# The last stage of a graph kernel: who weights the expert outputs, when they are loaded back, and what is prepared before the gathers arrive

## The chip, the core and the metric

The kernel runs on one core of a Trainium2 chip. Its engines work side by side and meet through semaphores: TensorE (PE in the profile; PEld is its weight load), VectorE (DVE), ScalarE (ACT), GpSimd (POOL), and SyncE (SP), which here issues plain DMAs. The metric is the time of the whole launch on the device in microseconds (us), lower being better. Before the change it is 2686.47 us, the median of 3 runs (2683.16 to 2688.34).

## What is computed

The reference is a two-layer graph network with 3125 nodes of 256 values each. Each layer is a graph convolution beside an attention-like mixer, and then a feed-forward part with experts. The change lies in the last part of the second layer, where four experts are weighted by a gate that comes from a second graph attention:

```python
def _L1_ffn_ref(x, W_gat, att_src, att_dst, b_gat, ln_gamma, ln_beta, W1, b1, W2, b2, edge_index):
    ...
        ee = jnp.exp(e - e_max[dst])
        denom = jax.ops.segment_sum(ee, dst, num_segments=M)
        alpha = ee / (denom[dst] + 1e-16)
        msg = h[src] * alpha[:, :, None]
        agg = jax.ops.segment_sum(msg, dst, num_segments=M).reshape(M, HEADS * NUM_EXPERTS) + b_gat
        scores = _layernorm(agg, ln_gamma, ln_beta).reshape(M, HEADS, NUM_EXPERTS).mean(1)
        ...
        topk_s, topk_i = jax.lax.top_k(scores, TOP_K)
        w = jax.nn.softmax(topk_s, axis=-1)
        out = jnp.zeros_like(x)
        for ei in range(NUM_EXPERTS):
            g = jnp.where(topk_i == ei, w, 0.0).sum(-1)
            hh = jax.nn.gelu(x @ W1[ei] + b1[ei], approximate=False)
            out = out + g[..., None] * (hh @ W2[ei] + b2[ei])
        return out
...
    x = x + _L1_ffn_ref(_layernorm(x, axis=-1)[None], ...)[0]
```

So at the end every node has four expert outputs of 256 values, a gate of four numbers (two of them zero), and its old value `x`; the result is `x` plus the gated sum.

## The kernel before

**Tiles.** The 3125 nodes are 25 tiles of 125 rows (`P`, `NT`). The tiles are handled in seven chunks, `CHUNKS`: four of four tiles and three of three. `self.x` holds all of `x` on chip for the whole kernel.

**Ahead of the tail.** `layer1_ffn` computes the four experts one after the other (`expert`, L1704). The outputs of experts 0 and 1 stay on chip (`y[0]`, `y[1]`, the second in the memory of `acc`); those of experts 2 and 3 are stored to `yd` in DRAM. Beside the experts, the segment sums of the graph attention are made by scans over the sorted edges and stored to `sums` in DRAM. After the last expert a short dependent piece (L1819 to L1856) works out what is carried from one partition to the next and leaves it in `taken`.

**The tail, L1859 to L1914,** has these parts:

- Loads (L1864 to L1868): for each of the seven chunks, a tile `yback` gets the outputs of experts 2 and 3 from `yd`. `move` (L63) splits each transfer in two DMAs, of 112 and 13 partitions, so there are 28 DMAs, all on SP's queue, into seven buffers.
- Gathers (L1869): 25 indirect DMAs by GpSimd, one per tile, fetch each node's row of 24 numbers from `sums` into `rs` (called `g_r` in the profile).
- Gates (L1872, and `graph_gates`, L1987): small VectorE operations over all tiles of a group at once, with three trips to ScalarE (exponentials, square root, exponential). There are three groups: chunks 0 and 1 (8 tiles), chunks 2 and 3 (8 tiles), chunks 4 to 6 (9 tiles). Before each group, TensorE fills `more` with the carried parts, one product per tile (L1877). `graph_gates` is a generator and yields at each trip to ScalarE, so that other work can be put there.
- Totals (L1881): `total(k, gate, ta)` adds the gated expert outputs of chunk k to `x`, and stores the chunk. It does so in two ways. Tiles at even places in the chunk are done by VectorE with four operations `x = out * gate + x` (L1889). Tiles at odd places are done by TensorE: an identity product brings `x` into PSUM (L1895), ScalarE makes four diagonal matrices with the gate on the diagonal (L1897), TensorE multiplies each with one expert's output onto the same PSUM tile (L1899), and ScalarE copies the result back to `x` (L1900). With four-tile chunks that is two and two, with three-tile chunks two and one: 14 tiles for VectorE, 11 for TensorE and ScalarE.

**The order.** TensorE, VectorE and ScalarE run in the order in which the Python code issues instructions (`manual_schedule`, L1904); SP and GpSimd are placed by the framework's scheduler. The order on each of these three is thereby fixed. The loop at L1906 issues a group's gates, and at each yield one total of the group before: while group 1's gates wait for ScalarE, chunks 0 and 1 are totalled; during group 2's gates, chunks 2 and 3; chunks 4, 5 and 6 follow at the end. ScalarE's queue is thus, for each round: two exponentials, the diagonals and copies of one chunk, square root (with its table load), the diagonals and copies of the next chunk, exponential (with its table load).

**Buffers.** `yback` has one buffer per chunk, `diag` three, the PSUM tile `fph` three. DMAs of SP use eight semaphores in turn, so that each waits until the one eight before it has landed; the gathers likewise.

Of the kernel before, what the change touches and what calls it, by code (L numbers as in the profile page):

```python
# [8 lines left out]
F32 = mybir.dt.float32  # L9
# [3 lines left out]
OP = mybir.AluOpType  # L13
# [5 lines left out]
D = 256  # L19
P = 125  # L20
NT = 25
CHUNKS = ((0, 4), (4, 4), (8, 4), (12, 4), (16, 3), (19, 3), (22, 3))
# [23 lines left out]
BIG = 1e30  # L46
# [3 lines left out]
def gather(nc, out, table, idx):  # L50
    nc.gpsimd.indirect_dma_start(  # L51
        out=out, out_offset=None, in_=table,
        in_offset=bass.IndirectOffsetOnAxis(ap=idx, axis=0))
# [9 lines left out]
def move(queue, out, in_):  # L63


    for s in (slice(0, 112), slice(112, P)):
        queue.dma_start(out[s], in_[s])
# [7 lines left out]
def rows_of(table):  # L75
    return table.rearrange("(t p) d -> p t d", p=P)
# [12 lines left out]
class Kernel:  # L89
# [1564 lines left out]
    def layer1_ffn(self):  # L1654
        nc, tc, a = self.nc, self.tc, self.a
        NE, FC = 4, 4
        R = 24
        C = 25
        with ExitStack() as c:
            big = c.enter_context(tc.tile_pool(name="f1", bufs=1))  # L1660
            ps_a = c.enter_context(tc.tile_pool(name="f1pa", bufs=2, space=PSUM))
# [5 lines left out]
            vec = {n: self.bcast(big, "L1_ffn_" + n) for n in ("b_gat", "ln_gamma", "ln_beta")}  # L1667
            srow = big.tile([P, NT, 20], F32, name="srow")
            row = big.tile([P, NT, 5], F32, name="row0")
            loop = big.tile([P, NT, 4], F32, name="loop")  # L1670
            tabg = self.dram.tile([N, 20], F32, name="tabg")
            tie = self.ties(big, NE, "s")
# [5 lines left out]
            ends = big.tile([128, N], F32, name="g_ends")  # L1678
# [122 lines left out]
            with tc.manual_schedule(engines={mybir.EngineType.DVE}):  # L1801
                step = -(-EC // (NE * len(CHUNKS)))
                sources(3 * step)
                for ei in range(NE):
                    if ei > 0:
                        w = weights(ei)
                    for t0, n in CHUNKS:
# [3 lines left out]
                        done = ei * len(CHUNKS) + CHUNKS.index((t0, n)) + 1  # L1811
# [41 lines left out]
            taken = big.tile([128, C], F32, name="g_taken")  # L1853
# [7 lines left out]
            ga = c.enter_context(tc.tile_pool(name="f1m", bufs=2))  # L1861
            rs = ga.tile([P, NT, R], F32, name="g_r", bufs=1)
            backs = []
            for t0, n in CHUNKS:  # L1864
                back = ga.tile([P, 2, 4, D], F32, name="yback", bufs=len(CHUNKS))
                for i in range(2):
                    move(nc.sync, back[:, i, :n, :], rows_of(yd[i])[:, t0:t0 + n, :])
                backs.append(back)  # L1868
            for t in range(NT):  # L1869
                gather(nc, rs[:, t, :], sums[:], self.seg_at[:, 1, t:t + 1])  # L1870

            def gates(c0, c1):  # L1872

                ta, tb = CHUNKS[c0][0], CHUNKS[c1 - 1][0] + CHUNKS[c1 - 1][1]
                more = ps_a.tile([P, 16, C], F32, name="ln_pt")
                for t in range(ta, tb):
                    nc.tensor.matmul(more[:, t - ta, :], ends[:, t * P:(t + 1) * P], taken, start=True, stop=True)  # L1877
                for gate in self.graph_gates(ga, ta, tb, rs, more[:, :tb - ta, :], loop, srow, vec, tie):
                    yield gate, ta

            def total(k, gate, ta):  # L1881

                t0, n = CHUNKS[k]
                for t in range(t0, t0 + n):
                    outs = [y[ei][:, t, :] if ei < 2 else backs[k][:, ei - 2, t - t0, :] for ei in range(NE)]
                    xs = self.x[:, t, :]
                    if (t - t0) % 2 == 0:
                        for ei in range(NE):
                            nc.vector.scalar_tensor_tensor(xs, outs[ei], gate[:, t - ta, ei:ei + 1], xs,  # L1889
                                                           op0=OP.mult, op1=OP.add)  # L1890
                        continue

                    diag = ga.tile([P, NE, P], F32, name="diag", bufs=3)
                    pm = ps_h.tile([128, 4 * P], F32, name="fph")[:P, :D]
                    nc.tensor.matmul(pm, self.ident[:P, :P], xs, start=True, stop=False)  # L1895
                    for ei in range(NE):
                        nc.scalar.activation(diag[:, ei, :], self.ident[:P, :P], AF.Copy,  # L1897
                                             scale=gate[:, t - ta, ei:ei + 1])
                        nc.tensor.matmul(pm, diag[:, ei, :], outs[ei], start=False, stop=(ei == NE - 1))  # L1899
                    nc.scalar.copy(xs, pm)  # L1900
                move(nc.sync, rows_of(self.out)[:, t0:t0 + n, :], self.x[:, t0:t0 + n, :])


            with tc.manual_schedule(engines={E_.PE, E_.DVE, E_.Activation}):  # L1904
                ready = []
                for c0, c1 in ((0, 2), (2, 4), (4, 7)):  # L1906
                    for gate in gates(c0, c1):
                        if gate[0] is None and ready:
                            total(*ready.pop(0))
                    while ready:  # L1910
                        total(*ready.pop(0))
                    ready = [(k, *gate) for k in range(c0, c1)]
                for r in ready:
                    total(*r)  # L1914
# [69 lines left out]
            if c in beside:  # L1984
                beside[c]()

    def graph_gates(self, ga, ta, tb, rs, more, loop, srow, vec, tie):  # L1987

        nc = self.nc
        NE, n, s = 4, tb - ta, slice(ta, tb)
        r, loop = rs[:, s, :], loop[:, s, :]
# [3 lines left out]
        nc.vector.tensor_scalar(m, m, 0.0, None, op0=OP.max)  # L1997
        nc.vector.tensor_mul(m, m, hasb)
        nc.vector.tensor_add(m, m, loop)
        none = ga.tile([P, n], F32, name="g_none2", bufs=1)  # L2000
        nc.vector.tensor_scalar(none, more[:, :, 24], BIG, -BIG, op0=OP.mult, op1=OP.add)
        c3 = ga.tile([P, n, 4], F32, name="g_c3", bufs=1)
        nc.vector.tensor_add(c3, more[:, :, 20:24], none[:, :, None].to_broadcast([P, n, 4]))
        nc.vector.tensor_tensor(m, m, c3, OP.max)
        nc.vector.tensor_sub(c3, c3, m)
        nc.scalar.activation(c3, c3, AF.Exp)
# [43 lines left out]
        nc.vector.tensor_add(agg, agg, all_tiles(vec["ln_beta"]))  # L2050
        sc = ga.tile([P, n, NE], F32, name="s_sc", bufs=1)
        nc.vector.tensor_reduce(sc, agg.rearrange("p t (h e) -> p t e h", h=4), AX.X, OP.add)
        nc.vector.tensor_scalar(sc, sc, 0.25, None, op0=OP.mult)
        gate = self.softmax_parts(ga, sc, NE, "s")
        yield None
        mask = self.top_two(ga, sc, NE, "s", tie, 9)
# [48 lines left out]
```

## Time and profile before

| | |
|---|---|
| median of 3 runs | 2686.47 us (2683.16 to 2688.34) |
| profiled execution | 3054.7 us |
| span of its trace, first to last instruction | 3053.0 us |
| busy: PE, VectorE, ScalarE, GpSimd | 2260.7, 1511.2, 570.1, 1635.4 us |
| mean granted clock of TensorE | 0.847 |
| VectorE totals, L1889 (`yback` form) | 28 operations, 485 ns each |
| diagonals on ScalarE, L1897 | 44 operations, 388 ns busy each; four in 1.27 us when back to back |
| copies on ScalarE, L1900 | 11 operations, 372 ns each |
| table loads of ScalarE in the tail | 1283 ns each |
| gathers of `g_r`, L51 | 25, 1.2 us of GpSimd each, one every 1.5 us |

The profiled execution is longer than a plain run by some 370 us, so times of the trace are compared with its own span. In a timeline row the first number is the start in us from the beginning of the span, the second the duration, then engine, line, operation, output and inputs; the bracket tells how long the engine had been idle and what ended that, as inferred from semaphores. In a table of windows the columns are the window, its length, busy time (and instructions) of PE, PEld, VectorE, ScalarE and GpSimd, the granted share of TensorE's clock, the busy share of the DMA engines, and GB/s.

The tail, from the first gather on, in stretches of a few us:

```profile
2962.00:2970.00 8.00, 6.07 (x34) 5.34 (x34) 0.00 (x0) 0.00 (x0) 5.96 (x5) 0.61 0.88 194
2970.00:2978.00 8.00, 0.00 (x0) 0.00 (x0) 0.00 (x0) 0.00 (x0) 6.17 (x7) 0.50 1.16 212
2978.00:2986.00 8.00, 0.00 (x0) 0.00 (x0) 2.97 (x16) 1.75 (x3) 6.46 (x6) 0.50 1.16 211
2986.00:2994.00 8.00, 0.00 (x0) 0.00 (x0) 6.84 (x29) 1.81 (x3) 6.47 (x6) 0.50 1.06 200
2994.00:3002.00 8.00, 3.79 (x10) 2.88 (x10) 7.12 (x27) 1.87 (x7) 5.28 (x5) 0.54 0.28 24
3002.00:3018.00 16.00, 10.96 (x49) 8.30 (x48) 13.44 (x54) 8.07 (x21) 0.00 (x0) 0.89 0.23 66
3018.00:3037.00 19.00, 12.74 (x40) 9.20 (x40) 16.75 (x56) 9.53 (x27) 0.00 (x0) 0.82 0.18 52
3037.00:3053.00 16.00, 6.84 (x28) 5.01 (x28) 11.11 (x24) 4.68 (x15) 0.00 (x0) 0.88 0.26 75
```

Until 2994 the DMA engines are full. From 2982 to the end VectorE is busy most of the time.

### The profile page before, as it was taken

Reading aid. Unit: us, or ns where it says so; the run is one execution under the profiler, and the core shown is the slowest. Engines: PE = TensorE matmul, PEld = TensorE weight load, DVE = VectorE, ACT = ScalarE, POOL = GpSimd, SP = SyncE. Lnnn points to the kernel's source line nnn. Section 1 sums busy time; section 2 is a strip of 40 time slices with the busy share of each in tenths; the row PEclk is TensorE's granted clock in tenths of the full one; section 3 lists DMA queues with packets and bytes.
Section 4 is the critical chain, followed back from the end, with each engine's and each line's share of the span. In section 5 each row is a group of like instructions: output and inputs, shape, how many; then the busy total and the mean of one; then the engine's idle time right before and its main releaser. Section 6 shows DMA issues by size and latency. Waiting matters only on the chain. (4 is left out here: it accounts for less than half of the span.)

```text
span 3053.0 us, 26728 instructions
## 1 busy us (share of the span) xinstructions
PE 2260.7 (74%) x9047; PEld 1671.3 (55%) x9047; DVE 1511.2 (49%) x3578; ACT 570.1 (19%) x1193; POOL 1635.4 (54%) x1486
## 2 busy tenths in 40 slices
PE   1762652239999769969999966999777685788884
PEld 1541531128767636658888854666565563455553
DVE  7875940035655595112212156998877730122237
ACT  1420000000000112112222233444100131122233
POOL 5887877720000035056666617778877465565612
PEclk9855765559999689979999978999898777889897
DMA  8904300030333012145555461111111210112134
GB/s 307 378 29 96 85 21 1 0 72 19 95 82 104 29 36 62 45 144 178 178 178 178 158 172 46 49 48 47 47 49 48 69 31 6 22 27 51 43 81 92
DMA packets 176285, 259.81 MB, mean 85 GB/s; under 512 B 54057, under 2 KB 141075, under 8 KB 172748
## 3 DMA queue, kind: packets, MB, share of 16 engines
q1 hardware_dynamic: 117947, 201.64, 21.8%
q0 software_dynamic: 52288, 47.17, 6.6%
q10 hardware_dynamic: 5894, 9.09, 0.9%
q8 instruction: 76, 1.25, 0.2%
q14 instruction: 80, 0.66, 0.1%
HBM read 173.99 MB, written 83.69 MB: 84 GB/s over the span
## 5 line engine op out<-in xcount | busy, mean ns | idle before, releaser
L58 POOL DMA_INDIRECT adj<-ch_sum,ch_place x391 | 484.3, 1239 | 149.9 <-issue 121.0
L51 POOL DMA_INDIRECT g<-tab,t_src x391 | 456.7, 1168 | 119.4 <-issue 110.2
L460 PE MATMUL psum<-sup,adjT 125*125 125x256 f32 x1250 | 326.8, 410 | 221.8 <-issue 180.6
L460 PEld LDWEIGHTS psum<-sup,adjT 125*125 125x125 f32 x1250 | 249.5, 202 | 288.4 <-issue 199.3
L51 POOL DMA_INDIRECT G<-tabg,g_src x256 | 253.4, 990 | 160.8 <-DVE g_src L1691 87.5
L58 POOL DMA_INDIRECT sorted<-s_rows,pos x256 | 245.1, 957 | 174.1 <-DVE s_rows L1059 104.6
L1293 PE MATMUL pw<-v,hot 128*125 128x260 f32 x1244 | 307.1, 407 | 0.0
L1293 PEld LDWEIGHTS pw<-v,hot 128*125 128x125 f32 x1244 | 244.5, 200 | 43.7
L866 PE MATMUL ph<-xs,w 128*128 128x256 f32 x960 | 220.5, 388 | 45.7 <-issue 38.9
L1717 PE MATMUL fpy<-fw,fh 128*125 128x256 f32 x800 | 202.8, 409 | 58.9 <-ACT fh L1711 29.1
L463 DVE TENSOR_TENSOR x<-x,psum 125x512 f32<-125x512 f32 (+1 forms) x104 | 68.8, 664 | 332.7 <-remote 136.9
L866 PEld LDWEIGHTS ph<-xs,w 128*128 128x128 f32 x960 | 183.3, 194 | 82.7 <-issue 50.5
L1717 PEld LDWEIGHTS fpy<-fw,fh 128*125 128x125 f32 x800 | 159.8, 203 | 108.1 <-issue 43.7
L894 PE MATMUL py<-w,h 128*128 128x256 f32 x960 | 216.7, 379 | 0.0
L1709 PE MATMUL fph<-xT,fw 128*128 128x500 f32 (+1 forms) x448 | 182.8, 559 | 33.4 <-issue 33.4
L620 POOL MEMSET tier<- 125x64 f32 x1 | 0.2, 157 | 380.6 <-PE psum L460 380.6
L894 PEld LDWEIGHTS py<-w,h 128*128 128x128 f32 x960 | 180.1, 190 | 23.3
L868 ACT ACTIVATE h<-ph,b 128x256 f32<-128x256 f32 x240 | 113.2, 473 | 386.3 <-PE ph L866 318.5
L1034 PE MATMUL pctx<-s_mv,s_ro 128*128 128x256 f32 x512 | 154.5, 413 | 1.9 <-DVE s_mv L1033 1.9
L170 ACT ACTIVATE ln_rs<-ln_mv,eps 125x4 f32<-125x4 f32 (+1 forms) x14 | 3.5, 293 | 790.0 <-DVE ln_mv L169 789.9
L1709 PEld LDWEIGHTS fph<-xT,fw 128*128 128x128 f32 x448 | 87.4, 197 | 110.0 <-issue 87.1
L1711 ACT ACTIVATE fh<-fph,cols 128x500 f32<-128x500 f32 (+1 forms) x112 | 69.8, 632 | 366.9 <-PE fph L1709 237.5
(551 smaller groups left out, 3500.8 us busy)
## 6 DMA issues: line engine op xcount, KB each, us to landing
adjT<-adj SPq DMA_DIRECT2D x25, 1367.2 KB
adj<-zero SPq DMA_DIRECT2D x22, 1536.0 KB
w<-in_L_ffn_W1p_dram SPq DMA_DIRECT2D x30, 1024.0 KB
w<-in_L_ffn_W2p_dram SPq DMA_DIRECT2D x30, 1024.0 KB
slots<-empty SPq DMA_DIRECT2D x1, 8448.0 KB
srow<-slots SPq DMA_DIRECT2D x30, 264.0 KB
adj<-ch_sum,ch_place POOLq DMA_INDIRECT x391
g<-tab,t_src POOLq DMA_INDIRECT x391
```

Source lines behind the costliest of these rows:

```text
L51: nc.gpsimd.indirect_dma_start(out=out, out_offset=None, in_=table, in_offset=bass.IndirectOffsetOnAxis(ap=idx, axis=0))
L58: return nc.gpsimd.indirect_dma_start(out=table, out_offset=bass.IndirectOffsetOnAxis(ap=idx, axis=0), in_=rows, in_offset=None, **kw)
L460: nc.tensor.matmul(pm[:, i, :], mats[b][:, (a0 + i) * P:(a0 + i + 1) * P], sup[:, b, :], start=(b == b0), stop=(b == b0 + n - 1))
L463: nc.vector.tensor_add(xs, xs, pm[:, :m, :])
L866: nc.tensor.matmul(ph, w1[:, k, f * 128:(f + 1) * 128], xs[:, k, :], start=(k == 0), stop=(k == 1))
L868: nc.scalar.activation(h[:, f, :], ph, AF.Gelu, bias=b1[:, f:f + 1])
L894: nc.tensor.matmul(py, h[:, f, i * 128:(i + 1) * 128], w2[:, f, :], start=(f == 0), stop=(f == FC - 1))
L1034: nc.tensor.matmul(p1, ro[:, f - f0, :], mv, **st)
L1293: nc.tensor.matmul(pw.rearrange("p h c -> p (h c)"), hot[:, i - i0, :], v[:, i, :, :].rearrange("p h c -> p (h c)"), start=(i == i0), stop ...
L1709: nc.tensor.matmul(ph[:, :n * P], w1[:, k, f * 128:(f + 1) * 128], xT[:, k, t0 * P:(t0 + n) * P], start=(k == 0), stop=(k == 1))
L1711: nc.scalar.activation(hs[:, f, :n * P], ph[:, :n * P], AF.Gelu, bias=self.col("L1_ffn_b1", ei * FC + f))
L1717: nc.tensor.matmul(py, hs[:, f, i * P:(i + 1) * P], w2[:, f, :], start=(f == 0), stop=(f == FC - 1))
```

## The change

1. **Split of the totals.** VectorE takes the first tile of each chunk, and in chunks 5 and 6 also the third; all others go to TensorE and ScalarE. That is nine tiles for VectorE and 16 for the others, where it was 14 and 11.
2. **Copies later.** Within a chunk, ScalarE copies a TensorE tile back only after it has issued the next tile's diagonals; what is left is copied at the end of the chunk. `diag` has four buffers.
3. **Loads in turn.** Only chunks 0 to 2 are loaded at first, `yback` has three buffers, and chunk k + 3 is loaded at the end of `total(k)`. In SP's queue the first load of chunk 3 stands before the store of chunk 0 and the other three behind it, and so on.
4. **Prepared scores.** The 25 products of `more` are made at once into two PSUM tiles, and what L2000 to L2003 did in each group (`none` and `c3`) is done for all tiles ahead of the gates, into `top`.
5. **The factor 0.25** of the scores (L2053) is put into `ln_gamma` and `ln_beta`, once.

```diff
@@ -1861,47 +1861,73 @@
             ga = c.enter_context(tc.tile_pool(name="f1m", bufs=2))
             rs = ga.tile([P, NT, R], F32, name="g_r", bufs=1)
             backs = []
-            for t0, n in CHUNKS:
-                back = ga.tile([P, 2, 4, D], F32, name="yback", bufs=len(CHUNKS))
+
+            def load(k):
+                t0, n = CHUNKS[k]
+                back = ga.tile([P, 2, 4, D], F32, name="yback", bufs=3)
                 for i in range(2):
                     move(nc.sync, back[:, i, :n, :], rows_of(yd[i])[:, t0:t0 + n, :])
                 backs.append(back)
+
+            for k in range(3):
+                load(k)
             for t in range(NT):
                 gather(nc, rs[:, t, :], sums[:], self.seg_at[:, 1, t:t + 1])
 
             def gates(c0, c1):
 
                 ta, tb = CHUNKS[c0][0], CHUNKS[c1 - 1][0] + CHUNKS[c1 - 1][1]
-                more = ps_a.tile([P, 16, C], F32, name="ln_pt")
-                for t in range(ta, tb):
-                    nc.tensor.matmul(more[:, t - ta, :], ends[:, t * P:(t + 1) * P], taken, start=True, stop=True)
-                for gate in self.graph_gates(ga, ta, tb, rs, more[:, :tb - ta, :], loop, srow, vec, tie):
+                more, at = carried[0 if c1 <= 4 else 1]
+                for gate in self.graph_gates(ga, ta, tb, rs, more[:, ta - at:tb - at, :], top[:, ta:tb, :], loop,
+                                             srow, vec, tie):
                     yield gate, ta
 
             def total(k, gate, ta):
 
                 t0, n = CHUNKS[k]
+                done = []
                 for t in range(t0, t0 + n):
                     outs = [y[ei][:, t, :] if ei < 2 else backs[k][:, ei - 2, t - t0, :] for ei in range(NE)]
                     xs = self.x[:, t, :]
-                    if (t - t0) % 2 == 0:
+                    if t == t0 or (k > 4 and t == t0 + 2):
                         for ei in range(NE):
                             nc.vector.scalar_tensor_tensor(xs, outs[ei], gate[:, t - ta, ei:ei + 1], xs,
                                                            op0=OP.mult, op1=OP.add)
                         continue
 
-                    diag = ga.tile([P, NE, P], F32, name="diag", bufs=3)
+                    diag = ga.tile([P, NE, P], F32, name="diag", bufs=4)
                     pm = ps_h.tile([128, 4 * P], F32, name="fph")[:P, :D]
                     nc.tensor.matmul(pm, self.ident[:P, :P], xs, start=True, stop=False)
                     for ei in range(NE):
                         nc.scalar.activation(diag[:, ei, :], self.ident[:P, :P], AF.Copy,
                                              scale=gate[:, t - ta, ei:ei + 1])
                         nc.tensor.matmul(pm, diag[:, ei, :], outs[ei], start=False, stop=(ei == NE - 1))
-                    nc.scalar.copy(xs, pm)
+
+                    done.append((xs, pm))
+                    if len(done) > 1:
+                        nc.scalar.copy(*done.pop(0))
+                for d in done:
+                    nc.scalar.copy(*d)
                 move(nc.sync, rows_of(self.out)[:, t0:t0 + n, :], self.x[:, t0:t0 + n, :])
+                if k + 3 < len(CHUNKS):
+                    load(k + 3)
 
 
             with tc.manual_schedule(engines={E_.PE, E_.DVE, E_.Activation}):
+
+                carried, top = [], ga.tile([P, NT, 4], F32, name="g_top", bufs=1)
+                none = ga.tile([P, NT], F32, name="g_none2", bufs=1)
+                for ta, tb in ((0, CHUNKS[4][0]), (CHUNKS[4][0], NT)):
+                    more = ps_a.tile([P, 16, C], F32, name="ln_pt")
+                    for t in range(ta, tb):
+                        nc.tensor.matmul(more[:, t - ta, :], ends[:, t * P:(t + 1) * P], taken, start=True, stop=True)
+                    nc.vector.tensor_scalar(none[:, ta:tb], more[:, :tb - ta, 24], BIG, -BIG, op0=OP.mult, op1=OP.add)
+                    nc.vector.tensor_add(top[:, ta:tb, :], more[:, :tb - ta, 20:24],
+                                         none[:, ta:tb, None].to_broadcast([P, tb - ta, 4]))
+                    carried.append((more, ta))
+
+                for v in ("ln_gamma", "ln_beta"):
+                    nc.vector.tensor_scalar(vec[v], vec[v], 0.25, None, op0=OP.mult)
                 ready = []
                 for c0, c1 in ((0, 2), (2, 4), (4, 7)):
                     for gate in gates(c0, c1):
@@ -1984,7 +2010,7 @@
             if c in beside:
                 beside[c]()
 
-    def graph_gates(self, ga, ta, tb, rs, more, loop, srow, vec, tie):
+    def graph_gates(self, ga, ta, tb, rs, more, c3, loop, srow, vec, tie):
 
 
 
@@ -1997,10 +2023,6 @@
         nc.vector.tensor_scalar(m, m, 0.0, None, op0=OP.max)
         nc.vector.tensor_mul(m, m, hasb)
         nc.vector.tensor_add(m, m, loop)
-        none = ga.tile([P, n], F32, name="g_none2", bufs=1)
-        nc.vector.tensor_scalar(none, more[:, :, 24], BIG, -BIG, op0=OP.mult, op1=OP.add)
-        c3 = ga.tile([P, n, 4], F32, name="g_c3", bufs=1)
-        nc.vector.tensor_add(c3, more[:, :, 20:24], none[:, :, None].to_broadcast([P, n, 4]))
         nc.vector.tensor_tensor(m, m, c3, OP.max)
         nc.vector.tensor_sub(c3, c3, m)
         nc.scalar.activation(c3, c3, AF.Exp)
@@ -2050,7 +2072,6 @@
         nc.vector.tensor_add(agg, agg, all_tiles(vec["ln_beta"]))
         sc = ga.tile([P, n, NE], F32, name="s_sc", bufs=1)
         nc.vector.tensor_reduce(sc, agg.rearrange("p t (h e) -> p t e h", h=4), AX.X, OP.add)
-        nc.vector.tensor_scalar(sc, sc, 0.25, None, op0=OP.mult)
         gate = self.softmax_parts(ga, sc, NE, "s")
         yield None
         mask = self.top_two(ga, sc, NE, "s", tie, 9)
```

## The prediction

> **Where the time goes now.** I read the page's first line, then the chain of waits cut to the last 90 us, because the diff touches nothing earlier and the order of instructions before the tail is the same in both kernels.
>
> ```profile
> span 3053.0 us, 26728 instructions
> ```
> ```profile
> by line: POOL g_r L51 23.3%; DVE x L1889 20.4%; PE fph L1899 11.0%; issue 9.7%; DMA g_r<-sums,g_ati 5.8%; ACT L653 2.8%; PE fph L1895 1.8%; DVE agg L2023 1.3%; DVE g_own L2019 1.1%; DVE g_den L2030 0.8%; ACT x L1900 0.8%; DVE agg L2032 0.7%
> ```
>
> So the tail (2960 to 3053) is first a queue of gathers (L51), then VectorE's totals (L1889), with TensorE's in between. The whole tail is 3% of the time: this change can move a few us, not tens. The timeline gives the stages:
>
> ```profile
> 2973.38 1.21 POOL L51 DMA_INDIRECT g_r<-sums,g_ati  x1 [0.31 <-issue]
> ...
> 2982.37 0.19 DVE L1996 TENSOR_TENSOR g_m<-g_r,loop 125x32 f32<-125x32 f32 x1 [20.60 <-DMA yback<-yd]
> ...
> 2997.39 0.48 DVE L1889 SCALAR_TENSOR_TENSOR x<-y,sm_exs,x 125x256 f32<-125x256 f32 x1
> ...
> 3004.52 0.37 ACT L1900 COPY x<-fph 125x256 f32<-125x256 f32 x1 [1.22 <-PE fph L1899]
> 3004.91 1.28 ACT L2045 ACT_TABLE_LOAD   x1
> ...
> 3006.44 0.30 ACT L2045 ACTIVATE s_mu<-s_mu,eps 125x8 f32<-125x8 f32 x1 [0.24 <-DVE s_mu L2044]
> ...
> 3018.08 0.48 DVE L1889 SCALAR_TENSOR_TENSOR x<-y,sm_exs,x 125x256 f32<-125x256 f32 x1
> ...
> 3036.91 0.48 DVE L1889 SCALAR_TENSOR_TENSOR x<-y,sm_exs,x 125x256 f32<-125x256 f32 x1
> ```
>
> VectorE stands idle 20.6 us until the first eight gathers are in (the releaser is inferred; L1996 reads only `g_r` and `loop`). Then come gate group 0 with the start of group 1 (15.0 us to 2997.39), round 1 (to 3018.08, 20.7 us), round 2 (to 3036.91, 18.8 us) and the last totals (to 3048.75, 11.8 us), then 4.3 us of stores. In the rounds ScalarE is only just in time: its table load for the square root ended at 3006.19, 0.2 us before VectorE had the input. That slack is the main thing to see: moving tiles to TensorE and ScalarE spends it.
>
> The second view is busy time and granted clock (the column after POOL) in windows of 3.41 us, the grid on which the clock changes here:
>
> ```profile
> 2997.96:3001.38 3.42, 3.17 (x8) 2.52 (x9) 3.24 (x8) 1.02 (x4) 2.24 (x2) 0.50 0.24 10
> 3001.38:3004.79 3.41, 3.08 (x14) 2.15 (x12) 3.07 (x15) 1.80 (x6) 0.00 (x0) 1.00 0.02 1
> 3004.79:3008.20 3.41, 1.25 (x6) 1.00 (x6) 3.13 (x10) 2.85 (x7) 0.00 (x0) 1.00 0.53 150
> 3008.20:3011.61 3.41, 3.41 (x10) 2.23 (x9) 3.17 (x10) 1.53 (x5) 0.00 (x0) 0.50 0.00 0
> ...
> 3035.51:3038.92 3.41, 1.50 (x7) 1.33 (x8) 2.70 (x9) 1.69 (x6) 0.00 (x0) 1.00 0.46 131
> ```
>
> TensorE at 1.25 of 3.41 us busy loses half its clock in the next window; at 1.50 (3035.51) it keeps it; a full window restores it. A pass of 256 columns takes 0.427 us at clock 0.50 and 0.215 at 1.00 (four `yback` passes from 3003.46 to 3004.32).
>
> **The change, part by part**
>
> *Head: loads in turn.* All 28 loads of `yback` are queued at once now, and the gathers share the DMA engines with them (1.16 busy, 212 GB/s from 2970 to 2978). A gather is 32 packets of queue 0 (800 for 25). By 2978, 194 had passed, six gathers, where POOL had issued ten; by 2996, with the loads over, 669, or 21 of 22. So a gather lands some 7 us behind its issue under the loads and 2 us without. Afterwards twelve loads are queued: 3.0 MB at 212 GB/s from 2963.5 end near 2978. The eighth gather, issued by 2974.6, then lands near 2979: **-3.0 us**. Ends: 0 (loads still thick around the eighth) and -5 (no lag but 2 us).
>
> *Head: less VectorE work before s.* L2001 and L2003 leave the gate groups (0.29 us of spacing in group 0, 0.31 in group 1), and L2053 goes (0.21): **-0.8**. In their place stand six VectorE operations and all 25 matmuls of `more` in front; they lie under the 20.6 us wait, and would cost 1.3 us if that were gone. Nine of those matmuls were 2.0 us of TensorE at 3012.68, beside other work: nothing saved. Head in all -3.8.
>
> *Rounds.* Each of chunks 0 to 3 loses one VectorE tile (four operations, 1.96 us) and gains a TensorE tile (four diagonals of ScalarE, 1.27, a copy, 0.37, ten passes). VectorE's part of round 1 falls from 20.7 to 16.3 us (two tiles, 0.31, 0.21). ScalarE and TensorE now decide. Their path: VectorE done to diagonal 0.34, to first pass 0.46, three tiles A, copy to table load 0.39, load to square root 1.30, to diagonal 0.20, to pass 0.46, three tiles B, 0.39, load to exponential 1.30, to L2057 0.26, to the next L1996 1.06, its first part 1.67: 7.8 + A + B.
>
> The copy behind the next diagonals lets three tiles stream: 28 passes (the first identity product is done ahead) at 0.215 and 0.3 to the copy: 6.3 us at full clock. Then the round is 20.4, no loss. But TensorE stands idle 5 us before A, so A starts at half clock, and only a window that is full nearly throughout restores it: 1 to 2 windows, 5.1 us, half of it lost, 2.55. Between A and B it stands idle 2.1 us. Here rule and row differ. The Trainium skill (TensorE: Matmul & The Clock Gate, section "What's actually happening") has the clock halved after at least one idle window of about 3.4 us; by that, B stays at 6.3. The row at 3004.79 halves it after 2.2 us of idling. I take the row: since 5.1 us of half clock leave A some 16 passes, it ends 3 to 4 us after a window's edge, and the pause falls mostly in one window, and B loses half a window, 1.7. The same page's section on warm-up has 3.4 us at half clock; this would make A's loss 1.7, not 2.55; again I take the rows.
>
> Round 1: 7.8 + 8.85 + 8.0 = 24.7, **+4.0**. Round 2 ends at the gates instead (6.0 + 16.85 = 22.9 against 18.8): **+4.1**. Ends: -0.3 each with the clock full throughout, +5 with both restarts in bad places.
>
> The copy also waits where nothing stood behind it: at a chunk's end the last copy waits for TensorE, and behind it in ScalarE's queue stand table load and square root (or exponential) for which VectorE waits.
>
> *Last totals.* VectorE falls from six tiles (11.84) to five (9.9). TensorE has four tiles: 0.5, 18 passes 4.2, copy and new diagonal 0.7, 2.0, 0.7, 2.0, copy 0.4: 10.6 at full clock. The pause ahead of it is 3.2 us, above the 2.2 of the row; some 5 us at half clock cost 2.4: 13.0, **+1.2** (ends -1.3, +2).
>
> *SP's queue.* Sixteen of the 28 loads now stand behind or between the stores of chunks 0 to 3, and each waits until three chunks back is read. The tightest is chunk 6: its first load follows chunk 3's last read, a store of 0.5 MB and three more loads; at 0.35 us an issue, 200 GB/s and 2 us to land it is in 6.5 us after, and is first read 9.8 us after (2.9 to the gates' end, 6.9 of totals). Cost 0 while that slack of 3 us lasts. Four `diag` buffers cost nothing that the trace shows.
>
> **Sum:** -3.8 + 4.0 + 4.1 + 1.2 = **+5.5 us**. The profiled execution took 3054.7 us (span 3053.0), so 3060.2 in its own terms. The runs' median of 2686.47 lacks the profiler's 368 us; the tail's clock and engine rows should hold in both, so I carry the 5.5 over unscaled: **2692 us**.
>
> **Rivals**
>
> 1. *No change that can be told* (0.2% either way, 5.4 us, is about what can be told here): the pause before B splits over two windows and the clock holds, as at 3035.51. Then B is 6.3 twice: +5.5 - 3.4 = +2.1, 2688.6. For: 2.1 us is at the edge of what the rows show. Against: A's end is tied to a window's edge.
> 2. *Faster.* TensorE keeps its clock through the tail, because its work is denser: rounds -0.3 and -0.2, last totals -1.2, head -3.8: -5.5, 2681. It decides once pauses stay under some 1.9 us in any window. Against: 5 us idle between rounds.
> 3. *Head gives nothing*: the first twelve loads hold the eighth gather back as before; +8.5, 2695.
> 4. *A load comes late*: chunk 6 three us or more beyond its slack, +3: 2695.
> 5. *Another bottleneck stays*: VectorE still decides. Its 16.3 us against 20.4 at best speaks against; the time would be near rival 2.
>
> **Numbers.** My forecast 0.44, half of it above the bound of 5.4 us: 0.22 slower, 0.22 no change. Rival 1: 0.19, no change. Rival 2 with 5: 0.10, faster. Rival 3: 0.17 and rival 4: 0.10, slower. Slower 0.49, same 0.41, faster 0.10. Range 2683 to 2698: from short of rival 2 to head without gain and a late load at once.
>
> **What would show it.** First L1996 near 2979. VectorE waiting in the rounds: some 2.7 us for each square root (8.95 us of its own against 11.7) and 6 for the exponential, where it waited 0.4 and 1.0. Half clock at the start of each round and after each pause between A and B. The last event a ScalarE copy, not L1889. Wrong if VectorE still waits under 2 us in a round, if the clock holds, or if the first L1996 has not moved.

## The result and the profile after

| | before | after |
|---|---|---|
| first comparison, median of 7 runs each | 2686.47 us (2683.16 to 2691.88) | 2697.48 us (2693.63 to 2701.11) |
| ratio, 95% interval | | 1.0041 [1.0028, 1.0053] |
| ratio of a second comparison (51 and 22 runs) | | 1.0024 [1.0016, 1.0031] |

The change makes the kernel slower by 6.5 to 11 us. The profile after is of an execution of 2699.8 us, close to the median:

```profile
span 2698.0 us, 26829 instructions
```

The trace of before that the prediction was read from came from an execution some 365 us longer for reasons ahead of the tail. A second trace of the unchanged kernel before (run e1) has a span of 2687.1 us, so it is used here beside the first. To compare tails, I count from the start of L1855, the operation that fills `taken`, on VectorE: everything in the tail waits for it.

Timeline rows of the kernel after (columns as before; L1894 is the totals' operation on VectorE, L2022 the first of a gate group, formerly L1889 and L1996):

```profile
2619.16 0.19 DVE L2022 TENSOR_TENSOR g_m<-g_r,loop 125x32 f32<-125x32 f32 x1 [7.12 <-DMA g_r<-sums,g_ati]
...
2633.51 0.48 DVE L1894 SCALAR_TENSOR_TENSOR x<-y,sm_exs,x 125x256 f32<-125x256 f32 x1
...
2642.95 0.37 ACT L1910 COPY x<-fph 125x256 f32<-125x256 f32 x1 [1.79 <-PE fph L1904]
2643.34 1.28 ACT L2067 ACT_TABLE_LOAD   x1
2644.64 0.30 ACT L2067 ACTIVATE s_mu<-s_mu,eps 125x8 f32<-125x8 f32 x1
2644.97 0.20 DVE L2069 RECIPROCAL s_mu<-s_mu 125x8 f32<-125x8 f32 x1 [2.45 <-ACT s_mu L2067]
...
2657.99 0.48 DVE L1894 SCALAR_TENSOR_TENSOR x<-y,sm_exs,x 125x256 f32<-125x256 f32 x1
...
2680.36 0.48 DVE L1894 SCALAR_TENSOR_TENSOR x<-y,sm_exs,x 125x256 f32<-125x256 f32 x1
...
2693.48 0.37 ACT L1910 COPY x<-fph 125x256 f32<-125x256 f32 x1 [1.22 <-PE fph L1904]
```

The starts of L1894 at 2633.51, 2657.99 and 2680.36 cut the tail into the prediction's stages: head, round 1 (24.48 us), round 2 (22.37), last totals (13.49, to 2693.85). In the middle of round 1 a ScalarE copy waits 1.79 us for TensorE, behind it come the table load and the square root, and VectorE stands idle 2.45 us until that is done. In the rounds of before VectorE never waits for the root: in round 1 of the first trace ScalarE had it done at 3006.74 (3006.44 + 0.30), and VectorE, with the totals of chunk 1 in between, came to the reciprocal 3.5 us later (3.0 in e1), without an idle time before it:

```profile
3010.23 0.20 DVE L2047 RECIPROCAL s_mu<-s_mu 125x8 f32<-125x8 f32 x1
```

The same turn shows in the waits of VectorE in the tail (columns: engine, tile, line, what it waited for; us in total, times, longest). After:

```profile
DVE sm_exs L2078 <- ACT sm_exs L653: 13.1, 2, 6.7
DVE g_none L1924 <- PE ln_pt L1923: 10.1, 2, 6.7
DVE g_m L2022 <- DMA g_r<-sums,g_ati: 7.1, 1, 7.1
DVE s_mu L2069 <- ACT s_mu L2067: 4.7, 3, 2.4
```

Before, second trace:

```profile
DVE g_m L1996 <- DMA g_r<-sums,g_ati: 20.9, 2, 20.7
DVE s_mu L2047 <- ACT s_mu L2045: 0.4, 1, 0.4
...
DVE sm_exs L2057 <- ACT sm_exs L653: 0.3, 1, 0.3
```

In each of these traces 0.4 us of the wait for the square root belongs to the head (gate group 0). So before, VectorE waits 0.3 us in the two rounds together (1.7 in the first trace, all of it for the exponentials); after, it waits 13.1 us for the exponentials and 4.3 for the square roots. The fall of the first wait from 20.7 to 7.1 is not all gain: after, VectorE waits up to 6.7 us earlier in the head for the products of L1923, and part of the rest is spent on the prepared scores.

Windows by stage (head from L1855, round 1, round 2, rest; columns as before). Before, second trace, and then after:

```profile
2597.20:2632.90 35.70, 7.08 (x34) 6.39 (x34) 12.57 (x61) 3.79 (x7) 27.65 (x23) 0.52 1.00 188
2632.90:2652.90 20.00, 14.29 (x58) 10.91 (x58) 17.89 (x66) 9.71 (x26) 2.62 (x2) 0.84 0.23 54
2652.90:2671.00 18.10, 12.62 (x40) 9.15 (x40) 16.54 (x54) 9.49 (x25) 0.00 (x0) 0.81 0.19 53
2671.00:2687.10 16.10, 6.84 (x28) 5.01 (x28) 11.20 (x24) 4.71 (x15) 0.00 (x0) 0.89 0.26 75
```
```profile
2600.80:2633.50 32.70, 11.36 (x52) 10.66 (x52) 13.07 (x61) 3.81 (x7) 25.31 (x22) 0.51 0.54 102
2633.50:2658.00 24.50, 17.49 (x60) 13.95 (x60) 13.83 (x55) 12.78 (x36) 4.80 (x4) 0.78 0.39 100
2658.00:2680.40 22.40, 17.22 (x60) 13.76 (x60) 12.81 (x46) 12.55 (x35) 0.00 (x0) 0.80 0.36 100
2680.40:2698.00 17.60, 11.91 (x38) 8.91 (x38) 9.30 (x20) 6.24 (x20) 0.00 (x0) 0.79 0.38 110
```

The head is 3.0 us shorter. The rounds are 4.5 and 4.3 longer although VectorE has 4.1 and 3.7 us less to do in them: it is busy 57% of a round, where it was 90%. No other engine is full either. TensorE's granted clock is 0.78 to 0.80, so a good part of its 17 busy us is at half speed (the windows under e8 show where).

### The profile page after: what moved, and what is told of

It is laid out like the page before. It is cut to its first block, busy times and chain, and to the rows that moved or that the text cites. A ratio compares the mean times of both kernels' runs of the same rounds, so it can differ in the third digit from the quotient of the medians.

```text
span 2698.0 us, 26829 instructions
## 1 busy us (share of the span) xinstructions
PE 2212.6 (82%) x9097; PEld 1666.8 (62%) x9097; DVE 1500.9 (56%) x3555; ACT 578.8 (21%) x1218; POOL 1660.3 (62%) x1486
## 5 line engine op out<-in xcount | busy, mean ns | idle before, releaser
L58 POOL DMA_INDIRECT adj<-ch_sum,ch_place x391 | 505.3, 1292 | 149.2 <-issue 114.1
L460 PE MATMUL psum<-sup,adjT 125*125 125x256 f32 x1250 | 292.8, 393 | 52.0 <-DMA adjT<-adj 41.0
L460 PEld LDWEIGHTS psum<-sup,adjT 125*125 125x125 f32 x1250 | 240.9, 195 | 93.4 <-DMA adjT<-adj 38.9
L1717 PE MATMUL fpy<-fw,fh 128*125 128x256 f32 x800 | 183.6, 385 | 10.4 <-ACT fh L1711 6.4
L1717 PEld LDWEIGHTS fpy<-fw,fh 128*125 128x125 f32 x800 | 150.2, 189 | 48.6 <-ACT fh L1711 12.1
L1709 PE MATMUL fph<-xT,fw 128*128 128x500 f32 (+1 forms) x448 | 176.6, 545 | 0.0
L58 POOL DMA_INDIRECT slots<-rows,abi x50 | 73.9, 1479 | 99.1 <-DVE r_cum L948 84.1
L897 DVE TENSOR_SCALAR yo<-py,own 128x256 f32<-128x256 f32 x60 | 27.8, 481 | 191.2 <-PE py L894 191.2
L463 DVE TENSOR_TENSOR x<-x,psum 125x512 f32<-125x512 f32 (+1 forms) x104 | 68.8, 664 | 109.3 <-PE psum L460 109.2
```

What stands on the lines that cost most here:

```text
L58: return nc.gpsimd.indirect_dma_start(out=table, out_offset=bass.IndirectOffsetOnAxis(ap=idx, axis=0), in_=rows, in_offset=None, **kw)
L460: nc.tensor.matmul(pm[:, i, :], mats[b][:, (a0 + i) * P:(a0 + i + 1) * P], sup[:, b, :], start=(b == b0), stop=(b == b0 + n - 1))
L463: nc.vector.tensor_add(xs, xs, pm[:, :m, :])
L897: nc.vector.tensor_scalar(yo, py, own[:, i, 2:3], None, op0=OP.mult)
L1709: nc.tensor.matmul(ph[:, :n * P], w1[:, k, f * 128:(f + 1) * 128], xT[:, k, t0 * P:(t0 + n) * P], start=(k == 0), stop=(k == 1))
L1717: nc.tensor.matmul(py, hs[:, f, i * P:(i + 1) * P], w2[:, f, :], start=(f == 0), stop=(f == FC - 1))
```

## The experiments

The main question is whether the rounds are long because TensorE's work starts at half clock after each pause, or because ScalarE now has more diagonals and copies in a row ahead of each table load, whatever TensorE's clock. Beside it, each part of the change was put back alone. Tails are given as head (L1855 to round 1), round 1, round 2, last totals (to the last operation of the totals), and the whole tail from L1855 to the end of the span. The two traces of before:

| | head | round 1 | round 2 | last | tail |
|---|---|---|---|---|---|
| before, first trace | 35.80 | 20.69 | 18.83 | 11.84 | 91.39 |
| before, e1 | 35.71 | 20.00 | 18.14 | 11.84 | 89.92 |
| after, first trace | 32.72 | 24.48 | 22.37 | 13.49 | 97.26 |

### e1: the kernel before, again

> The kernel before, unchanged, for a second trace beside the others. Ratio 1.000 within 0.001. Theory (the tail's clock and ScalarE path): the tail, from the start of L1855 to the end of the span, is 91.4 us as in the first trace, so that of the measured 11 us only some 6 lie in the tail, and 5 are to be looked for ahead of L1855. Rival (the first trace of before, 355 us longer than a plain run, was drawn out in its tail too): the tail is 86 to 88 us, and explains all 11.

Ratio 1.0003 [0.9994, 1.0013]. The tail agrees with the first trace within 1.5 us; the 0.7 us less in each round is VectorE's wait for the exponential, 0.3 us once here against 1.7 us over two in the first trace. The tail's 89.92 us lies between the theory's 91.4 and the rival's 86 to 88.

### e2: after, with the old split of the totals

```diff
-                    if t == t0 or (k > 4 and t == t0 + 2):
+                    if (t - t0) % 2 == 0:
```

> The changed kernel with the old split of tiles (14 and 11), all else kept. Theory (the split costs, the rest gains): head -3.1 us as in the changed kernel, rounds again set by VectorE and 0.5 and 0.2 shorter for L2001, L2003 and L2053, last totals 11.8 as before: -3.8 us, 2682.7, ratio 0.9986. Rival (loads in turn, or the prepared scores, cost time): ratio 1.002 or more.

Ratio 0.9991 [0.9982, 1.0001]. Stages 32.70, 19.30, 18.70, 11.84; tail 86.75. The rounds are those of before again, the head keeps its gain. So the loss sits in the split, and everything else in the change together is worth 3.2 to 4.6 us of tail, which the time shows at best as a tendency.

### e3: before, with the new split alone

```diff
-                    if (t - t0) % 2 == 0:
+                    if t == t0 or (k > 4 and t == t0 + 2):
```

> The kernel before with the new split alone (9 and 16), copies at once, loads at once. Theory: no gain at the head; three tiles with a copy in between cost 1.0 us more a chunk than streamed ones, so each round takes 2 us longer than in the changed kernel: +5.8 and +5.5, last totals +1.7: +13 us, 2699.5, ratio 1.0048. Rival (the split is not the cause): 1.000 to 1.002.

Ratio 1.0051 [1.0035, 1.0067]. Stages 35.67, 27.03, 24.85, 11.17; tail 102.91. The split by itself costs 6.0 to 7.0 us in each round; in the first trace of after the other parts of the change give 2.5 us of each back, and 3 in the head, but the last totals take 2.3 more. The rounds were expected 5.8 and 5.5 us longer; the last totals, expected 1.7 longer, came out 0.7 shorter than before, with TensorE at full clock from 2679.9 on.

### e4: after, with all loads at once

```diff
-                back = ga.tile([P, 2, 4, D], F32, name="yback", bufs=3)
+                back = ga.tile([P, 2, 4, D], F32, name="yback", bufs=len(CHUNKS))
...
-            for k in range(3):
+            for k in range(len(CHUNKS)):
                 load(k)
...
-                if k + 3 < len(CHUNKS):
-                    load(k + 3)
```

> The changed kernel with all 28 loads queued at the start into seven buffers. Theory: the gain of 2.4 us at the first gate is lost, the rest stays: 2699.9, ratio 1.005. Rival (loads behind the stores cost time that the trace of the tail does not show): faster than the changed kernel, 2692, ratio 1.002.

Ratio 1.0020 [1.0013, 1.0028], not told from the 1.0024 that after has in another comparison (e8). The theory's 1.005 was missed, and the figure is the rival's; whether for the rival's reason, no trace shows. Stages 34.46, 22.08, 22.69, 13.64; tail 97.07. The gates start 20.50 us after L1855 and not 18.38: loads in turn are worth 2.1 us there and 1.7 at the head's end. Round 1 was shorter than in the first trace of after for another reason: the clock was not lost in its middle, as in e8.

### e5: after, with TensorE kept busy in its pauses

This run tells the two theories apart. TensorE gets products into a scratch PSUM tile that nobody reads, in the pauses ahead of and between the chunks' work. ScalarE's queue is untouched. A first one waits for `sq`, a tile of the gates, so that they do not run too early.

```diff
+            FILL = {2: (4, 11), 4: (4, 6)}
+            scratch = ps_y.tile([P, D], F32, name="fpy")
+
+            def busy(n, after=None):
+
+                if after is not None:
+                    nc.tensor.matmul(scratch[:, :128], self.ident[:P, :P], after[1], start=True, stop=True)
+                for _ in range(n):
+                    nc.tensor.matmul(scratch, self.ident[:, :P], ends[:, :D], start=True, stop=True)
+
...
-                    for gate in gates(c0, c1):
+                    for i, gate in enumerate(gates(c0, c1)):
+                        if c0 == 0 and i == 1:
+                            busy(10, after=gate[2])
...
+                            busy(FILL[c0][i])
```

> The changed kernel with products whose result nobody reads, put into TensorE's pauses: 10 ahead of round 1, 4 between the two chunks of a round, 11 and 6 behind a round. Theory (half clock after the pauses makes the rounds long): the clock holds from round 1 on, rounds fall from 24.5 and 22.4 us to 20.4 and 18.6, last totals from 13.5 to 10.6: tail 86.5 us from L1855 to the end instead of 97.3, ratio 0.9987. Rival (the added passes and the copies cost by their number, not by the clock): rounds of 24 us or more, since TensorE only has more to do; ratio 1.004 or above.

Ratio 0.9987 [0.9981, 0.9994], against 1.0024 for after in the same comparison: some 10 us less, and 3.5 less than before. Stages 32.63, 20.63, 18.63, 10.58; tail 86.65. The two rounds by windows:

```profile
2633.30:2654.00 20.70, 20.50 (x95) 17.31 (x94) 13.88 (x56) 12.78 (x36) 4.79 (x4) 1.00 0.48 122
2654.00:2672.60 18.60, 17.98 (x82) 14.84 (x80) 12.68 (x45) 12.56 (x35) 0.00 (x0) 1.00 0.41 113
```

ScalarE does exactly what it did in after (36 instructions, 12.78 us in round 1), TensorE has 35 passes more, and the round is 3.85 us shorter at clock 1.00. Had ScalarE's chain set the length whatever the clock, the round would have stayed at after's length. That theory falls. (The old split with the same filling, e11 below, is no shorter than without it, so the added passes do nothing for a round that VectorE sets.)

VectorE's waits in e5 show what is left:

```profile
DVE sm_exs L2091 <- ACT sm_exs L653: 9.7, 2, 5.0
...
DVE s_mu L2082 <- ACT s_mu L2080: 0.4, 1, 0.4
```

The wait for the square root is gone from the rounds (the 0.4 us is the head's), that for the exponential is some 4.9 us a round: with the clock held, VectorE has room to take a tile back.

### e6: after, with each copy at once

```diff
-                    done.append((xs, pm))
-                    if len(done) > 1:
-                        nc.scalar.copy(*done.pop(0))
-                for d in done:
-                    nc.scalar.copy(*d)
+                    nc.scalar.copy(xs, pm)
```

> The changed kernel with each tile copied back at once instead of behind the next diagonals. Theory: TensorE pauses at each copy, 0.5 us a tile, and warms up later: rounds 27.0 and 24.9 us as with the split alone, tail about 100 us, ratio 1.004, some 3 us above the changed kernel beside it. Rival (the later copy is what delays ScalarE's table loads): rounds shorter than 24.5 and a time below the changed kernel.

Ratio 1.0026 [1.0017, 1.0036]; after itself, in the same comparison, 1.0024: no difference in time. Stages 32.66, 26.70, 24.86, 11.17; tail 99.58. The rounds (26.7 and 24.9 us) and the tail are those expected and longer than in either trace of after, the last totals shorter. But the expected ratio of 1.004 was missed, and as a measure of time it is inconclusive.

### e7: filled, and VectorE takes 11 tiles

```diff
-                    if t == t0 or (k > 4 and t == t0 + 2):
+                    if t == t0 or (t == t0 + 2 and k not in (0, 2, 4)):
```

(on top of e5: two tiles for VectorE in the second chunk of each round and in chunks 5 and 6, one in the others. That is 11 tiles for VectorE and 14 for TensorE, as the trace has it, with 22 totals on `yback` at L1904; the 12 and 13 of the expectation below are a slip in counting.)

> The filled kernel with 12 tiles on VectorE and 13 on TensorE: one VectorE tile in chunks 0, 2 and 4, two in the others. Theory: with the clock held, one chunk of three and one of two TensorE tiles make rounds of 18.3 and 16.5 us, last totals 10.6; tail 82.3 us, ratio 0.9972. Rival (VectorE or the gathers set the end again): rounds of 19 us and more, ratio 0.9985 or above.

Ratio 0.9970 [0.9959, 0.9981], some 8 us faster than before. Stages 32.70, 18.70, 16.47, 10.58; tail 82.64. Windows of the two rounds, and VectorE's wait for the exponential:

```profile
2630.00:2648.70 18.70, 18.50 (x85) 15.47 (x84) 15.55 (x59) 11.24 (x31) 4.77 (x4) 1.00 0.54 137
2648.70:2665.20 16.50, 15.69 (x71) 12.99 (x70) 14.56 (x50) 11.02 (x30) 0.00 (x0) 1.00 0.47 127
```
```profile
DVE sm_exs L2091 <- ACT sm_exs L653: 1.7, 2, 1.1
```

The 9.7 us of waiting of e5 are 1.7 here. This version beats both kernels.

### e8: after, again

> The changed kernel again, timed beside the three above. Theory: its tail of 97.3 us against 89.9 in the clean trace of before is the whole effect: +7.3 us, ratio 1.0027, below the first ratio but inside its interval. Rival (something ahead of L1855 costs 4 us more): 1.004 again.

Ratio 1.0024 [1.0016, 1.0031]. Stages 32.66, 22.15, 22.89, 12.07; tail 93.95. Round 1 is 2.3 us shorter than in the first trace of after, with the same code. Of this, 0.6 us lies ahead of the square root's table load (9.20 us from the start of the round for 9.83; half clock lasts 3.4 us there for 4.7), and 1.7 us between square root and exponential. The windows on the clock's grid from the middle of round 1 show where the 1.7 come from:

```profile
2642.10:2645.52 3.42, 1.57 (x8) 1.03 (x6) 1.51 (x4) 2.21 (x5) 0.00 (x0) 1.00 0.22 51
2645.52:2648.93 3.41, 3.32 (x15) 2.92 (x16) 3.09 (x12) 3.36 (x13) 0.00 (x0) 1.00 1.03 335
```

The pause between the two chunks fell so that its window kept 1.57 us of work (46%), and the clock stayed. In the first trace of after it was 1.48 us (43%), and the next window ran at half clock:

```profile
2639.02:2642.43 3.41, 3.41 (x17) 2.95 (x17) 3.13 (x10) 0.99 (x4) 0.19 (x1) 1.00 0.08 4
2642.43:2645.84 3.41, 1.48 (x8) 0.96 (x7) 0.88 (x4) 2.86 (x7) 0.00 (x0) 1.00 0.43 136
2645.84:2649.26 3.42, 3.42 (x10) 2.69 (x9) 2.50 (x10) 2.09 (x8) 0.00 (x0) 0.50 0.97 301
2649.26:2652.67 3.41, 3.41 (x17) 2.98 (x16) 0.00 (x0) 1.23 (x4) 0.00 (x0) 1.00 0.06 17
```

The pause itself is as long in both, as the first pass behind it tells (first trace of after, then e8):

```profile
2645.28 0.70 PE L1904 MATMUL fph<-y,diag 125*125 125x256 f32 x2 [1.93 <-ACT diag L1902]
```
```profile
2645.61 0.70 PE L1904 MATMUL fph<-y,diag 125*125 125x256 f32 x2 [1.94 <-ACT diag L1902]
```

In the first trace the whole pause lies within the window that ends at 2645.84; in e8 its last 0.09 us lies behind the edge at 2645.52. In round 2 both traces lost the clock in this place.

So the prediction's forecast and its rival 1 (the clock held between the chunks) are both real: they are two outcomes of one kernel, decided by where the pause falls on the grid.

### e9, e10, e11: filled, with one part put back

The edits of e6, e4 and e2 on top of e5. These three were compared in a session in which the kernel before too ran at 3050 us, and the intervals are wide; so the traces of the tail serve.

> The filled kernel (new split) with each tile copied back at once. With the clock held, only the pauses at the copies are left. Theory: 0.5 us for each of the first two TensorE tiles of a chunk: rounds 22.7 and 20.7 us instead of 20.6 and 18.6, last totals 11.1, tail 91.4 us, ratio 1.0004. Rival (the later copy gains nothing by itself, only the clock did): rounds of 20.6 and 18.6 again, ratio 0.9987.

> The filled kernel (new split) with all 28 loads queued at once. Theory: the first gate starts 2 us later, the rest is as in the filled kernel: tail 88.5 us, ratio 0.9994. Rival (the loads in turn delay something later by as much as they gain at the head): 0.9987 again or below.

> The filled kernel with the old split of tiles (14 and 11). Theory: VectorE sets the rounds (19.2 and 18.4 us) and the last totals (11.8), so holding the clock brings almost nothing over the same kernel without filling (tail 86.75): 86.3 us, ratio 0.9989; the gain of the balanced version is then the split made possible by the clock. Rival (the filling alone is the gain): ratio 0.997.

| | ratio | head | round 1 | round 2 | last | tail |
|---|---|---|---|---|---|---|
| e5, filled | 0.9987 [0.9981, 0.9994] | 32.63 | 20.63 | 18.63 | 10.58 | 86.65 |
| e9, copies at once | 0.9998 [0.9980, 1.0016] | 32.76 | 23.02 | 21.01 | 11.17 | 92.15 |
| e10, all loads at once | 0.9992 [0.9972, 1.0011] | 34.45 | 20.83 | 18.63 | 10.58 | 88.69 |
| e11, old split | 0.9996 [0.9976, 1.0016] | 32.70 | 19.53 | 18.52 | 11.84 | 86.84 |

With the clock held, the later copies are worth 2.4 us in each round. ScalarE's waits for TensorE before a copy say where they come from, e9 first and then e5 (whose two lines are the copy beside the next diagonals, L1918, and that at a chunk's end, L1920):

```profile
ACT x L1916 <- PE fph L1914: 19.5, 16, 1.2
```
```profile
ACT x L1920 <- PE fph L1914: 11.4, 7, 1.8
ACT x L1918 <- PE fph L1914: 2.5, 4, 0.6
```

Sixteen waits of 1.2 us become seven at the chunks' ends and four short ones. Loads in turn are worth 1.8 us in the head, as in e4. The new split (e5 against e11) is worth nothing in the tail, 0.2 us: what it costs in round 1 it gains in the last totals. None of the three differences is resolved by the times.

### Tails and times together

Against the mean of the two tails of before (90.7 us), the tails of e2, e3, e4, e5, e6 and e7 are -3.9, +12.2, +6.4, -4.0, +8.9 and -8.0 us. The ratios, times the median of before, are -2.4, +13.7, +5.4, -3.5, +7.0 and -8.1 us. So what these parts do to the time is done in the tail, as far as single traces can tell. For after, the tails give +3.3 (e8) and +6.6 us, the ratios +6.5 and +11. About 3 to 4 us of after's loss are not in the tail of its traces. L1855 starts at 2600.8 and 2601.8 in them, against 2597.2 in e1, but in the other variants of after with the same order of instructions ahead it starts anywhere from 2595.5 to 2603.6. With one trace of each this stays open.

## Why the prediction was right, and where its sum was off

The forecast was 2692 us, with VectorE turning from the bound to waiting. The direction and the mechanism held, and 2697.48 us lies inside the range, near its upper end. That it lies inside is in part luck: the first trace of after has a tail 5.9 to 7.3 us longer than before's (that of e8 only 2.6 to 4.0), near the forecast 5.5, and the rest of the 11 us shows in no stage of the tail and answers to no step of the prediction. The range reached that far because of rivals 3 and 4, and neither came true. By its steps:

- **Head, loads in turn.** The mechanism was right: the first gate operation moved from 20.8 us after L1855 to 18.2–18.4, -2.4 to -2.7 for the predicted -3.0, and the opposite edit takes 2.1 back (e4) or 1.8 at the head's end (e10). The term was oversized by up to 0.6. From the first gate operation to round 1, where the small operations of the scores were saved, it is 14.3 to 14.5 us for 14.9 to 15.0: -0.4 to -0.7 for the predicted -0.8. Rival 3 (the head gives nothing) is ruled out.
- **ScalarE and TensorE decide the rounds.** As predicted: VectorE waits 2.45 us for the square root in round 1 for the predicted 2.7, 6.7 for the exponential for 6 (1.8 and 5.0 in e8). Rival 5 is out.
- **The slack.** The 0.2 us that the prediction calls the main thing is a misreading: it is the time from the end of the table load to the root's input, and VectorE needs the root only 3.5 us after it is done (L2047 above). Without slack was the exponential, for which VectorE waited 1.0 us already. In the rounds it waited for nothing else; the 0.4 us that the prediction names for the root is the head's. The sum didn't suffer, since it set ScalarE's path against VectorE's own 8.95 us.
- **A at half clock.** From the start of round 1 to the table load the first trace of after has 9.83 us; the path predicted 10.04 (0.34 + 0.46 + 8.85 + 0.39). Half clock lasts from A's first pass (2634.29) to the edge at 2639.02, 4.7 us for the predicted 5.1. In e8 it lasts 3.4 us (2635.25 to 2638.69) and the path 9.20 us, a loss near the 1.7 that the prediction set aside: how much is lost depends on where in a window A starts. e5, where the clock holds, brings the two rounds to 20.63 and 18.63, the prediction's own figures for full clock being 20.4 and 18.6 (its -0.3 and -0.2 on 20.7 and 18.8).
- **B at half clock after a short pause.** From the square root to the exponential's table load it was 9.06 us, as predicted (0.20 + 0.46 + 8.0 + 0.39 = 9.05). In round 1 of e8 it was 7.38, which is 1.7 less: the predicted price of the lost half window, not paid there. The row was taken over the Trainium skill's rule (TensorE: Matmul & The Clock Gate, section "What's actually happening"), which asks for an idle window of about 3.4 us. The row was right: a pause of 1.93 us within one window halved the clock. What did not hold as said is that A's end is tied to an edge closely enough to fix the place of the pause: it was to come 3 to 4 us behind an edge, and the pause begins 4.3 us behind the edge that restored the clock in the first trace (2639.02) and 5.0 in e8 (2638.69), where it reached into the next window.
- **Rounds.** 24.48 and 22.37 for 24.7 and 22.9 in the first trace, 22.15 and 22.89 in the second. As differences they are +3.8 and +3.5 against the first trace of before but +4.5 and +4.2 against e1: the baseline was read from one trace, in which VectorE waited 1.0 and 0.8 us at L2057. In the second trace of after round 1 is only 1.5 to 2.2 us longer than before.
- **Last totals.** 13.49 and 12.07 for 13.0, within its ends. When the clock holds they are 10.58, for 10.6.
- **Late loads** (rival 4). In neither trace of after does TensorE or VectorE wait for `yback` from the first round on; the slack of 3 us was enough.
- **The faster rival** (2, the clock holds, -5.5 us) was right about the price: e5 forced that case, and its tail is 3.3 to 4.7 us shorter than before's. It was rightly given a small chance, since nothing in the change holds the clock.

**What failed in the argument** is smaller: that the 368 us between trace and median are the profiler's. The profiled execution of e1 took 2688.81 us beside a median of 2689.26, so the profiler adds nothing that shows; and in the session of e9 to e11 plain runs of before took 3050 us too. In the first trace the time was spent ahead of the tail (the last operation of L463 starts at 1019.1, in e1 at 799.6), for a reason that stays open; the tail agrees with e1's within 1.5 us, so the sum stood. And what the forecast missed of the first measured +11 has no shown cause.

## What to carry to other kernels

Before moving work from an engine that is always busy to one with gaps, read in the rows what that engine does after a gap: here each pass of TensorE took twice as long after a pause, and the new path had no slack ahead of the exponential. Where the receiving engine's clock depends on how busy it is, give it something to do in its pauses first and rebalance after: the same split that cost 7 to 13 us of tail cost nothing with the pauses filled, and from there 11 tiles for VectorE and 14 for TensorE were the better balance of the three that ran (tail 82.64 us, for 86.65 with 9 and 86.84 with 14). And take a stage's baseline from two traces when the effect looked for is a few us.

## What was not expected of the hardware

**The clock is a step on a grid of 3.41 us, and the busy share read from a trace tells the step only nearly.** In all 13 traces the time between two changes of the granted clock is a whole number of windows of 3.413 us. From the start of the totals on, a window of up to 1.48 us of work (43%) lost the clock in the next window, and one of 1.49 us or more kept it, with two exceptions in the last passes of e3 (1.45 us) and e6, which kept it:

```profile
2697.12:2700.53 3.41, 1.48 (x7) 0.94 (x5) 0.56 (x2) 0.67 (x3) 0.00 (x0) 1.00 0.58 162
2700.53:2703.20 2.67, 0.00 (x0) 0.00 (x0) 0.00 (x0) 0.00 (x0) 0.00 (x0) 1.00 0.27 81
```

Ahead of the totals, with other products, the two cases overlap further: 1.58 us lost it in e8 (at 2133.52), 1.98 in after (1068.88) and 2.15 in the first trace of before (2960.41), while 1.40 kept it in e3 (1942.62). So between 41 and 63% the busy share alone doesn't settle it. Two traces of the same kernel, with nothing else different, thus part by 1.7 us in one round over 0.09 us of a pause.

**One nearly busy window is not always enough to get it back.** In the last totals of the kernel after:

```profile
2676.56:2679.98 3.42, 1.31 (x7) 0.79 (x5) 0.49 (x3) 1.89 (x3) 0.00 (x0) 1.00 0.41 100
2679.98:2683.39 3.41, 2.52 (x6) 2.04 (x7) 3.16 (x9) 2.42 (x8) 0.00 (x0) 0.50 0.91 278
2683.39:2686.80 3.41, 3.41 (x9) 2.64 (x9) 3.23 (x8) 0.37 (x1) 0.00 (x0) 0.50 0.00 0
2686.80:2690.22 3.42, 3.09 (x14) 2.38 (x14) 3.24 (x7) 1.54 (x5) 0.00 (x0) 1.00 0.28 76
```

The window from 2679.98 is busy 2.52 us (74%) at half clock, and the next is still at half; only the full one at 2683.39 restores it. Elsewhere in the totals up to 83% (2.83 us, e4 at 2680.69) did not restore it and 85% (2.91 us, e4 at 2636.32) did. So work that starts too late in a window to fill some 85% of it pays half clock until that window's end and for all of the next one. Nor is a full window always enough: in the head of the kernel after, TensorE is busy without a gap with the 50 passes of 25 columns of L1923, and the clock stays at half:

```profile
2604.88:2608.30 3.42, 3.42 (x18) 3.42 (x18) 0.40 (x2) 0.00 (x0) 2.81 (x3) 0.50 1.04 231
2608.30:2611.71 3.41, 3.41 (x16) 3.41 (x17) 0.19 (x2) 0.00 (x0) 2.80 (x3) 0.50 1.16 223
```

The restoring windows quoted here are all of passes of 256 columns; what sets the two apart no run here shows.
